# Small layernorm operations on GpSimd, paired feed-forward chunks, an earlier second load and a split last layernorm, in a two-layer graph network

## The chip, the cores and the metric

The kernel runs on one core of one Trainium2 chip. The metric is the device time of one execution in microseconds (us). The kernel before takes 3535.06 us, the median of three runs (3534.37 to 3538.44).

I call the engines by the short names that the profile uses: PE (TensorE, the matmuls), PEld (its weight loads), DVE (VectorE), ACT (ScalarE), POOL (GpSimd).

## The reference

The input is 128 graphs of 128 nodes with 256 features and an integer adjacency matrix each. Cut to what matters:

```python
def layer0(x, adj):
    h = gat(gat(x, adj, W1, a1), adj, W2, a2)      # two graph-attention steps: softmax over masked scores
    h = layernorm(x + h, g_ln1, b_ln1)
    ff = relu(h @ w_ff1 + b_ff1) @ w_ff2 + b_ff2    # 256 -> 1024 -> 256: the first feed-forward
    return layernorm(h + ff, g_ln2, b_ln2)

def layer1(src, adj):
    attn = softmax(q @ k.T / sqrt(32)) per head     # 8 heads, 4 relations that select values
    x = layernorm(src + attn_out @ Wo + bo, g1, beta1)
    ff = gelu(x @ W1 + b1) @ W2 + b2                # the second feed-forward
    return layernorm(x + ff, g2, beta2)
```

Everything is in float32. There are four layernorms per graph.

## The kernel before

The kernel works on 32 groups of four graphs and overlaps the stages of several groups: each stage is a generator, and a heap interleaves their steps by the begin and end times in a table. The build then orders the instructions of each engine by a simulated time, so the order on an engine is not simply the order of the text.

The layernorm of four graphs (128 calls in a run) takes its statistics on VectorE, `rstd` and `nmr` through three small operations that go from VectorE to GpSimd and back, and the scaling on ScalarE. The weights of the layernorm are applied by GpSimd, two operations for each pair of graphs (`affine`):

```python
def normalised(y):
    mv = sm.tile([P, G, 2], F32, name="mv")
    for b in range(G):
        st = sm.tile([P, 6], F32, name="st")
        nc.vector.bn_stats(st, y[:, b])
        nc.vector.bn_aggr(mv[:, b], st)
    rstd = sm.tile([P, G], F32, name="rstd")
    nc.vector.tensor_scalar(rstd, mv[:, :, 1], EPS, None, op0=OP.add)                                   # L166
    nc.gpsimd.tensor_tensor(rstd, rstd, mhalf, OP.pow)                                                  # L167
    nmr = sm.tile([P, G], F32, name="nmr")
    nc.vector.scalar_tensor_tensor(nmr, mv[:, :, 0], -1.0, rstd, op0=OP.mult, op1=OP.mult)              # L169
    for b in range(G):
        nc.scalar.activation(y[:, b], y[:, b], AF.Identity, bias=nmr[:, b:b + 1], scale=rstd[:, b:b + 1])  # L171

def affine(y, k, b):
    for op, v in zip((OP.mult, OP.add), ln[k][0]):
        nc.gpsimd.tensor_tensor(y[:, b:b + 2], y[:, b:b + 2], v[:, None, :].to_broadcast([P, 2, D]), op)   # L177
```

The feed-forward transposes its input, in two halves of 128 features. ScalarE writes the first half to `T` (L190) and VectorE the second (L188). Then come eight chunks of 128 hidden features, each with a matmul on either half (L202) into one accumulator tile "mm":

```python
def feed_forward(y, before, win, bin_, wout, func):
    hT = transposed(y, before)
    fT = []
    for f in range(FC):                                  # FC = 8
        p = ps.tile([P, T], F32, name="mm")
        for c in range(DC):                              # DC = 2, the halves
            nc.tensor.matmul(p, win[:, c, ts(f, P)], hT[:, c], start=c == 0, stop=c == DC - 1)   # L202
        t = wk.tile([P, T], F32, name="fT", tag="fT", bufs=FC + 1)
        nc.scalar.activation(t, p, func, bias=bin_[:, f:f + 1])                                  # L204
    ...                                                  # output matmuls (L214), add, normalised
```

Five accumulator tiles are called "mm", two "tr" and one "av": eight in all, each of 512 float32 columns or less. The Trainium skill ("PSUM — Partial Sum Buffer", the section "PSUM: the matmul accumulator") says that this is all there is, eight banks of 512 float32 values per partition.

Group 0's input is loaded among the first weights, group 1's behind all of them. The last group's output leaves in one piece, after the affine steps of all four graphs.

## Time and profile before

| | kernel before |
|---|---|
| time, median of 3 | 3535.06 us |
| span of the profiled run | 3533.7 us |
| PE busy | 3448.5 us (98%) |
| DVE, ACT, POOL busy | 49%, 48%, 31% |
| one group in the steady part | 108.02 us |

The last row is worked out from the trace: the distance between the first output matmuls (L214) of group 6's and of group 30's first feed-forward, over the 24 groups between (for these marks I count groups from 1; the code, and what I say of loading, counts from 0). With PE busy for 98% of the span, only its gaps can be won. The prediction below shows the lines for that. The two small operations that leave VectorE, each on its line of source; the columns are the count, then the shortest, median and longest duration in ns:

```profile
L166 DVE TENSOR_SCALAR rstd<-mv x128: 150/356/964, 43.8 to 3522.5; 128x4 f32<-128x4 f32 x128
L169 DVE SCALAR_TENSOR_TENSOR nmr<-mv,rstd x128: 133/164/1247, 45.1 to 3523.8; 128x4 f32<-128x4 f32 x128
```

Each is about 0.15 us of work at its shortest, and sometimes takes 1 us or more. The timeline of all engines shows such a case (start, duration, engine, line):

```profile
1082.43 1.28 POOL L177 TENSOR_TENSOR tok<-tok,ln_rows 128x512 f32<-128x512 f32 x1
1082.50 1.22 DVE L169 SCALAR_TENSOR_TENSOR nmr<-mv,rstd 128x4 f32<-128x4 f32 x1
```

The 4-column operation of VectorE begins just after GpSimd's large one and ends with it.

### The profile page before, as it was taken

Reading aid. Unit: us, or ns where it says so; the run is one execution under the profiler, and the core shown is the slowest. Engines: PE = TensorE matmul, PEld = TensorE weight load, DVE = VectorE, ACT = ScalarE, POOL = GpSimd, SP = SyncE. Lnnn points to the kernel's source line nnn. Section 1 sums busy time; section 2 is a strip of 40 time slices with the busy share of each in tenths; the row PEclk is TensorE's granted clock in tenths of the full one; section 3 lists DMA queues with packets and bytes.
Section 4 is the critical chain, followed back from the end, with each engine's and each line's share of the span. In section 5 each row is a group of like instructions: output and inputs, shape, how many; then the busy total and the mean of one; then the engine's idle time right before and its main releaser. Section 6 shows DMA issues by size and latency. Waiting matters only on the chain.

```text
span 3533.7 us, 52086 instructions
## 1 busy us (share of the span) xinstructions
PE 3448.5 (98%) x20496; PEld 2255.0 (64%) x20496; DVE 1720.9 (49%) x3781; ACT 1684.0 (48%) x4702; POOL 1091.0 (31%) x968
## 2 busy tenths in 40 slices
PE   7999999999999999999999999999999999999997
PEld 5566666666666666666666666666666666666655
DVE  2544445545455444455454554444554545544453
ACT  3455445555445554455554455544555544555442
POOL 2223323223233233232332332332323323323332
PEclk8999999999999999999999999999999999999999
DMA  4000000000000000000000000000000000000000
GB/s 177 7 10 22 22 22 16 7 22 22 22 16 13 16 22 22 22 16 7 22 22 22 16 11 18 22 22 22 16 7 22 22 22 10 9 8 7 7 7 13
DMA packets 23780, 70.86 MB, mean 20 GB/s; under 512 B 2416, under 2 KB 6000, under 8 KB 23408
## 3 DMA queue, kind: packets, MB, share of 16 engines
q1 hardware_dynamic: 23536, 67.53, 5.6%
q8 instruction: 162, 2.65, 0.3%
q14 instruction: 82, 0.67, 0.1%
HBM read 50.75 MB, written 16.78 MB: 19 GB/s over the span
## 4 chain that ended last, share of the span: by engine, by line
PE 85%; ACT 8%; DVE 5%; DMA 1%; issue 0%; POOL 0%; POOLq 0%; SPq 0%; ACTq 0%; DVEq 0%
PE mm L202 25%; PE mm L214 19%; PE mm L331 12%; PE av L343 7%; ACT kbd L286 5%; PE mm L246 3%; PE mm L277 3%; PE mm L370 3%; PE tr L318 3%; PE mm L295 2%; PE mm L255 2%; PE mm L264 2%; PE mm L283 2%; ACT e L233 1%; PE tr L186 1%; ACT tr L226 1%
## 5 line engine op out<-in xcount | busy, mean ns | idle before, releaser
L177 POOL TENSOR_TENSOR tok<-tok,ln_rows 128x512 f32<-128x512 f32 x512 | 640.2, 1276 | 442.8 <-PE tr L186 252.0
L322 DVE SCALAR_TENSOR_TENSOR m<-at,tr 128x512 f32<-128x512 int32 x1024 | 627.7, 678 | 93.6 <-PE tr L318 79.3
L307 POOL TENSOR_TENSOR e<-e,s 128x512 f32<-128x512 f32 x256 | 263.0, 1044 | 761.2 <-DVE mv L164 665.6
L204 ACT ACTIVATE fT<-mm,col 128x512 f32<-128x512 f32 x512 | 331.3, 686 | 339.4 <-PE mm L202 336.3
L202 PE MATMUL mm<-T,w 128*128 128x512 f32 x1024 | 476.0, 603 | 15.4 <-DVE T L188 14.8
L202 PE MATMUL mm<-T,wf 128*128 128x512 f32 x1024 | 471.1, 598 | 12.5 <-ACT T L190 12.5
L331 PE MATMUL mm<-wv,T 128*128 128x512 f32 x1024 | 461.0, 592 | 0.6 <-ACT e L305 0.6
L214 PE MATMUL mm<-w,fT 128*128 128x256 f32 x2048 | 460.3, 381 | 0.0
L214 PE MATMUL mm<-wf,fT 128*128 128x256 f32 x2048 | 456.0, 381 | 0.0
L171 ACT ACTIVATE tok<-tok,nmr,rstd 128x256 f32<-128x256 f32 x512 | 267.9, 611 | 377.2 <-DVE nmr L169 377.2
L215 DVE TENSOR_TENSOR tok<-tok,mm 128x512 f32<-128x512 f32 x128 | 88.0, 687 | 712.7 <-PE mm L214 712.7
L214 PEld LDWEIGHTS mm<-w,fT 128*128 128x128 f32 x2048 | 384.2, 190 | 69.4 <-issue 21.2
L214 PEld LDWEIGHTS mm<-wf,fT 128*128 128x128 f32 x2048 | 384.3, 190 | 57.1 <-issue 7.4
L305 ACT ACTIVATE e<-mm,nm 128x128 f32<-128x128 f32 x1024 | 358.6, 387 | 19.4 <-DVE nm L301 19.0
L202 PEld LDWEIGHTS mm<-T,w 128*128 128x128 f32 x1024 | 185.0, 190 | 234.4 <-issue 191.9
L202 PEld LDWEIGHTS mm<-T,wf 128*128 128x128 f32 x1024 | 184.6, 190 | 211.1 <-issue 184.0
L331 PEld LDWEIGHTS mm<-wv,T 128*128 128x128 f32 x1024 | 189.6, 190 | 203.3 <-issue 182.7
L235 POOL TENSOR_TENSOR e<-e,s 128x512 f32<-128x512 f32 x64 | 66.6, 1041 | 803.7 <-DVE s L234 803.7
L343 PEld LDWEIGHTS av<-m,v 128*32 128x32 f32 x8192 | 218.1, 110 | 70.8 <-issue 60.3
L167 POOL TENSOR_TENSOR rstd<-rstd,mhalf 128x4 f32<-128x4 f32 x128 | 130.2, 1017 | 430.9 <-DVE rstd L166 405.8
L343 PE MATMUL av<-m,v 128*32 128x128 f32 x8192 | 252.9, 276 | 7.8 <-DVE v L332 4.6
L347 ACT COPY oT<-av 128x256 f32<-128x256 f32 x128 | 47.0, 367 | 392.5 <-PE av L343 392.5
(62 smaller groups left out, 3897.9 us busy)
## 6 DMA issues: line engine op xcount, KB each, us to landing
xt<-in_xT_dram SPq DMA_DIRECT2D x32, 512.0 KB, 3.3
tok<-in_x_dram SPq DMA_DIRECT2D x32, 512.0 KB, 3.3
out_dram<-tok SPq DMA_DIRECT2D x32, 512.0 KB, 2.7
at<-in_adjT_dram SPq DMA_DIRECT2D x32, 256.0 KB, 2.8
wf<-in_wf_dram SPq DMA_DIRECT2D x2, 1024.0 KB, 10.6
w<-in_w_dram SPq DMA_DIRECT2D x2, 1024.0 KB, 13.0
ln_rows<-in_rows_dram SPq DMA_DIRECT2D x1, 1024.0 KB, 11.0
wv<-in_wv_dram SPq DMA_DIRECT2D x1, 1024.0 KB, 9.8
```

The costliest lines, as they stand in the source:

```text
L167: nc.gpsimd.tensor_tensor(rstd, rstd, mhalf, OP.pow)
L171: nc.scalar.activation(y[:, b], y[:, b], AF.Identity, bias=nmr[:, b:b + 1], scale=rstd[:, b:b + 1])
L177: nc.gpsimd.tensor_tensor(y[:, b:b + 2], y[:, b:b + 2], v[:, None, :].to_broadcast([P, 2, D]), op)
L202: nc.tensor.matmul(p, win[:, c, ts(f, P)], hT[:, c], start=c == 0, stop=c == DC - 1)
L204: nc.scalar.activation(t, p, func, bias=bin_[:, f:f + 1])
L214: nc.tensor.matmul(p[:, b - b2_], fT[f][:, ts(b, N)], wout[:, f], start=f == 0, stop=f == FC - 1)
L286: nc.scalar.activation(kbd[c][rows, :, q % 2], p[rows], AF.Identity, bias=bk[rows, c:c + 1])
L305: nc.scalar.activation(e[:, q], p[:, q], AF.Exp, bias=nm[:, q:q + 1], accum_out=s[:, q:q + 1])
L307: nc.gpsimd.tensor_mul(e, e, per_row(s, N))
L322: nc.vector.scalar_tensor_tensor(m, ab, r, pT, op0=OP.is_equal, op1=OP.mult)
L331: nc.tensor.matmul(p, hT[:, f, ts(b, N)], wv[:, f, r:r + 2], start=f == 0, stop=f == DC - 1)
L343: last = nc.tensor.matmul(po[ts(q, DH), c], v[:, r, c * P + q * DH:c * P + (q + 1) * DH], ms[q // 2][r][:, c * 2 + q % 2], start=r == R - ...
```

## The change

The intent, in four parts:

- **GpSimd:** all small operations of the layernorm go to GpSimd, so that VectorE no longer hands over and waits for the power.
- **Pairs:** the feed-forward takes its chunks by pairs, with the input half in the outer loop, so that two matmuls run on the first half before the second half is needed.
- **Loading:** the input of group 1 is loaded right behind the first weights.
- **End:** the last group is normalised and written out by two graphs at a time, with the affine steps on VectorE. In the same place the pauses (`yield 2`) before the affine steps of all other groups go too.

```diff
+    second_xt = ld.tile([P, DC, T], F32, name="xt")
+    nc.sync.dma_start(second_xt, xT[1])
...                                                   # at[1] beside it, x[1] before wf2; load_group from group 2 on
-    def normalised(y):
+    def normalised(y, first=0, n=G):
...
-        nc.vector.tensor_scalar(rstd, mv[:, :, 1], EPS, None, op0=OP.add)
-        nc.gpsimd.tensor_tensor(rstd, rstd, mhalf, OP.pow)
-        nmr = sm.tile([P, G], F32, name="nmr")
-        nc.vector.scalar_tensor_tensor(nmr, mv[:, :, 0], -1.0, rstd, op0=OP.mult, op1=OP.mult)
+        nc.gpsimd.tensor_scalar(rstd, mv[:, :, 1], EPS, None, op0=OP.add)
+        nmr = sm.tile([P, n], F32, name="nmr")
+        nc.gpsimd.tensor_scalar(nmr, mv[:, :, 0], -1.0, None, op0=OP.mult)
+        nc.gpsimd.tensor_tensor(rstd, rstd, mhalf[:, :n], OP.pow)
+        nc.gpsimd.tensor_mul(nmr, nmr, rstd)
...
-        for f in range(FC):
-            p = ps.tile([P, T], F32, name="mm")
+        for f0 in range(0, FC, 2):
+            pair = [ps.tile([P, T], F32, name="mm") for _ in range(2)]
             for c in range(DC):
-                nc.tensor.matmul(p, win[:, c, ts(f, P)], hT[:, c], start=c == 0, stop=c == DC - 1)
+                for i, p in enumerate(pair):
+                    nc.tensor.matmul(p, win[:, c, ts(f0 + i, P)], hT[:, c], start=c == 0, stop=c == DC - 1)
...
-        normalised(y)
+            if (b2_ + 2) % by == 0:                   # by = 2 in the last group's second feed-forward, else 4
+                normalised(y, b2_ + 2 - by, by)
...
+            affine(y, "12", b, nc.vector if last else nc.gpsimd)
+            if last:
+                nc.sync.dma_start(out[g][:, b:b + 2], y[:, b:b + 2])
...
-            if g == 1 and n < 2:
+            if g == 1 and n == 1:                     # group 1's first stage still begins 0.6 of a group early
```

More of the change, by code (lines that the diff above doesn't have):

```diff
@@ L106, in graph_layers @@
     nc.sync.dma_start(first_at, adjT[0])
+    second_xt = ld.tile([P, DC, T], F32, name="xt")
+    nc.sync.dma_start(second_xt, xT[1])
+    second_at = ld.tile([P, G, N], I32, name="at", bufs=4)
+    nc.sync.dma_start(second_at, adjT[1])
     first_x = wk.tile([P, G, D], F32, name="tok", bufs=KB)
     nc.sync.dma_start(first_x, x[0])
-    first_load = first_x, first_xt, first_at
     pa = ps.tile([P, DC, 2], F32, name="mm")
@@ L136, in graph_layers @@
           for n, k in enumerate(KS)}
+    second_x = wk.tile([P, G, D], F32, name="tok", bufs=KB)
+    nc.sync.dma_start(second_x, x[1])
     wf2 = wload("wf2")
@@ L156, in per_row @@
         return v[:, :, None].to_broadcast([P, v.shape[-1], n])
-    def normalised(y):
-        mv = sm.tile([P, G, 2], F32, name="mv")
-        for b in range(G):
+    def normalised(y, first=0, n=G):
+        y = y[:, first:first + n]
+        mv = sm.tile([P, n, 2], F32, name="mv")
+        for b in range(n):
             st = sm.tile([P, 6], F32, name="st")
@@ L164, in normalised, with affine @@
             nc.vector.bn_aggr(mv[:, b], st)
-        rstd = sm.tile([P, G], F32, name="rstd")
-        nc.vector.tensor_scalar(rstd, mv[:, :, 1], EPS, None, op0=OP.add)
-        nc.gpsimd.tensor_tensor(rstd, rstd, mhalf, OP.pow)
-        nmr = sm.tile([P, G], F32, name="nmr")
-        nc.vector.scalar_tensor_tensor(nmr, mv[:, :, 0], -1.0, rstd, op0=OP.mult, op1=OP.mult)
-        for b in range(G):
+        rstd = sm.tile([P, n], F32, name="rstd")
+        nc.gpsimd.tensor_scalar(rstd, mv[:, :, 1], EPS, None, op0=OP.add)
[3 more added lines that the diff above has]
+        nc.gpsimd.tensor_mul(nmr, nmr, rstd)
+        for b in range(n):
             nc.scalar.activation(y[:, b], y[:, b], AF.Identity, bias=nmr[:, b:b + 1], scale=rstd[:, b:b + 1])
-    def affine(y, k, b):
+    def affine(y, k, b, engine=nc.gpsimd):
         for op, v in zip((OP.mult, OP.add), ln[k][0]):
-            nc.gpsimd.tensor_tensor(y[:, b:b + 2], y[:, b:b + 2], v[:, None, :].to_broadcast([P, 2, D]), op)
+            engine.tensor_tensor(y[:, b:b + 2], y[:, b:b + 2], v[:, None, :].to_broadcast([P, 2, D]), op)
     def transposed(y, k):
@@ L191, in transposed, with feed_forward @@
         return t
-    def feed_forward(y, before, win, bin_, wout, func):
+    def feed_forward(y, before, win, bin_, wout, func, by=G):
         hT = transposed(y, before)
@@ L198, in feed_forward @@
         fT = []
-        for f in range(FC):
-            p = ps.tile([P, T], F32, name="mm")
+        for f0 in range(0, FC, 2):
+            pair = [ps.tile([P, T], F32, name="mm") for _ in range(2)]
             for c in range(DC):
-                nc.tensor.matmul(p, win[:, c, ts(f, P)], hT[:, c], start=c == 0, stop=c == DC - 1)
-            t = wk.tile([P, T], F32, name="fT", tag="fT", bufs=FC + 1)
-            nc.scalar.activation(t, p, func, bias=bin_[:, f:f + 1])
-            fT.append(t)
-            if f % 2:
-                yield 1
-                if f in (3, 5):
-                    affine(y, before, f - 3)
+                for i, p in enumerate(pair):
+                    nc.tensor.matmul(p, win[:, c, ts(f0 + i, P)], hT[:, c], start=c == 0, stop=c == DC - 1)
+            for i, p in enumerate(pair):
+                t = wk.tile([P, T], F32, name="fT", tag="fT", bufs=FC + 1)
+                nc.scalar.activation(t, p, func, bias=bin_[:, f0 + i:f0 + i + 1])
+                fT.append(t)
+            yield 1
+            if f0 in (2, 4):
+                affine(y, before, f0 - 2)
         for b2_ in range(0, G, 2):
@@ L376, in ff0, with ff1 @@
         return feed_forward(y, "01", wf1, bf1, wf2, AF.Relu)
-    def ff1(y):
-        return feed_forward(y, "11", w1, b1, w2, AF.Gelu)
-    x0, x1, x2, masks, loads = {}, {}, {}, {}, {0: first_load}
+    def ff1(y, by):
+        return feed_forward(y, "11", w1, b1, w2, AF.Gelu, by)
+    x0, x1, x2, masks, loads = {}, {}, {}, {}, {}
+    loads[0] = first_x, first_xt, first_at
+    loads[1] = second_x, second_xt, second_at
     def stage_load(g):
-        if g:
+        if g > 1:
             loads[g] = load_group(g)
@@ L399, in stage_ff1 @@
     def stage_ff1(g):
-        y = yield from ff1(x2.pop(g))
+        last = g == NG - 1
+        y = yield from ff1(x2.pop(g), 2 if last else G)
         for b in range(0, G, 2):
-            yield 2
-            affine(y, "12", b)
-        nc.sync.dma_start(out[g], y)
+            affine(y, "12", b, nc.vector if last else nc.gpsimd)
+            if last:
+                nc.sync.dma_start(out[g][:, b:b + 2], y[:, b:b + 2])
+        if not last:
+            nc.sync.dma_start(out[g], y)
     stages = ((stage_load, 1, -0.7, -0.6), (stage_gat, 11, 0.0, 0.5), (stage_ff0, 8.5, 0.65, 1.15),
```

## The prediction

> **What bounds the kernel now.** I read the page first, its engine totals:
>
> ```profile
> PE 3448.5 (98%) x20496; PEld 2255.0 (64%) x20496; DVE 1720.9 (49%) x3781; ACT 1684.0 (48%) x4702; POOL 1091.0 (31%) x968
> ```
>
> The matrix engine has work 98% of the time, the others at most half. All instructions that the change moves are on engines with room; they pay only where PE waits for them. PE is idle 3533.7 - 3448.5 = 85.2 us. Busy is not proof of full rate, so I next took the distance from one start to the next in the PE timeline:
>
> ```profile
> 1021.73 3.60 PE L331 MATMUL mm<-wv,T 128*128 128x512 f32 x8
> 1025.16 1.08 PE L186 MATMUL tr<-ident,tok 128*128 128x128 f32 x8
> 1026.63 2.84 PE L202 MATMUL mm<-T,wf 128*128 128x512 f32 x6 [0.39 <-ACT T L190]
> ```
>
> Eight 512-column instructions take 1025.16 - 1021.73 = 3.43 us, 0.429 us each; nearly all 512-column ones of the trace keep that pitch. (A feed-forward has 8 chunks x 2 halves x 32 groups = 512 matmuls and the trace 1024 instructions: two per matmul.) The change removes no matmul, so this rate is a floor, and only gaps can be won. Where they are, from the windows by stage:
>
> ```profile
> 0.00:54.00 54.00, 29.25 (x100) 22.55 (x101) 11.89 (x30) 20.14 (x62) 11.64 (x16) 0.81 0.79 290
> 54.00:215.00 161.00, 153.24 (x810) 101.43 (x808) 65.33 (x151) 68.72 (x190) 37.58 (x35) 0.98 0.03 9
> 215.00:3241.00 3026.00, 3000.78 (x17926) 1960.22 (x17922) 1508.27 (x3308) 1475.72 (x4123) 953.01 (x842) 1.00 0.05 17
> 3241.00:3486.00 245.00, 233.49 (x1562) 150.84 (x1562) 130.59 (x280) 107.73 (x311) 76.83 (x68) 1.00 0.02 7
> 3486.00:3534.00 48.00, 31.75 (x104) 19.97 (x104) 4.86 (x16) 11.71 (x18) 11.89 (x10) 0.84 0.03 11
> ```
>
> The second column is the length, the third PE's busy time, the third from the end its granted clock. Idle: start 24.8 us, filling 7.8, the 28 steady groups 25.2 (0.8%), emptying 11.5, end 16.3. And the list of waits of PE:
>
> ```profile
> PE mm L202 <- DVE T L188: 14.8, 29, 0.5
> PE mm L202 <- ACT T L190: 13.2, 32, 0.8
> PE tr L186 <- ACT tok L171: 8.6, 2, 5.3
> PE mm L255 <- POOL e L235: 6.0, 1, 6.0
> PE mm L246 <- DMA xt<-in_xT_dram: 5.3, 1, 5.3
> ```
>
> The two that repeat once per group are both the feed-forward's first matmuls, waiting for the transposed input: its first half comes from ScalarE (L190), its second from VectorE (L188). The change's outer loop over halves aims at these. The rest are single events of start and end.
>
> **What the skill says.** "TensorE: Matmul & The Clock Gate", Architectural detail: PE can pull a weight load ahead of running matmuls; its section on LDWEIGHTS gives columns / 1.2 GHz, 107 ns for 128. The trace agrees: where PE has stalled, the next instruction also comes 104 ns late (533 instead of 429 ns), so a stall costs its length and about one exposed load. Part 1 of that page: an idle array falls to half clock. Here the clock is 0.81 in the start and 0.84 in the end, so a shorter start gap is worth slightly more than itself. "SBUF — State Buffer", SBUF: two separate sides: VectorE with two SBUF inputs or in a two-port mode and GpSimd hold one port pair exclusively, the loser blocks. The trace is consistent: the 4-column VectorE operations of the layernorm take 0.17 us beside an idle GpSimd, but on average 0.469 (L166) and 0.665 us (L169). "GPSIMD Engine Reference", 4.1: elementwise is about 2x slower there; here 1.28 us for the 128x512 affine step, while VectorE adds 128x768 in 0.96 (L134).
>
> **The change, part by part.**
>
> *Pairs.* One steady group, from the timeline of all engines:
>
> ```profile
> 1079.23 0.66 DVE L301 TENSOR_REDUCE nm<-mm 128x4 f32<-128x512 f32 x1
> ...
> 1079.42 1.12 PE L202 MATMUL mm<-T,w 128*128 128x512 f32 x2
> ...
> 1079.80 0.50 DVE L166 TENSOR_SCALAR rstd<-mv 128x4 f32<-128x4 f32 x1
> ...
> 1080.21 0.80 DVE L188 TENSOR_SCALAR T<-tr,col 128x512 f32<-128x512 f32 x1
> ...
> 1081.07 2.84 PE L202 MATMUL mm<-T,w 128*128 128x512 f32 x6 [0.52 <-DVE T L188]
> ```
>
> The second feed-forward does one matmul on the first half, then needs the second, which VectorE evicts late, behind a maximum and the small L166. PE would have gone on at 1079.42 + 2 x 0.429 = 1080.28 (slightly later after its own exposed load, 0.10) and goes on at 1081.07: 0.69 us lost, and 0.10 after it, 0.79 per group. With pairs, a second matmul on the first half (2 x 0.429 = 0.86 us) comes before the second half is wanted, which covers all; and L166 leaves VectorE, so the half comes some 0.5 us earlier too. 30 groups x 0.79 = 24 us saved.
>
> The first feed-forward waits otherwise: for ScalarE's half, before its *first* matmul (the 1026.63 line above; 0.66 us with the exposed load after the last transpose). No loop order helps that. It also seems to run by pairs already: its second matmul starts at 1026.63 + 0.97 = 1027.60, while VectorE writes the second half from 1027.46 to 1028.23, so the build's scheduler must have put the next chunk's first-half matmul there. 0 us saved.
>
> *GpSimd.* 128 layernorms lose L166 and L169 from VectorE: 60.0 + 85.1 us of busy time and 118.8 us for which L169 held its queue waiting for the power. GpSimd gets three more 4-column operations, 384 in all. The trace has none except the power (1.02 us, a special function) and memsets (0.10 us); I estimate 0.15 us each, 58 us, 31% to 33% busy. The chain to ScalarE was 0.17 + 1.02 + 0.16 and two crossings, and becomes some 0.45 + 1.02 and one: equal. In the steady part PE does not wait for it: 0 us beyond the pairs' share.
>
> *Loading.* The PE timeline of the start:
>
> ```profile
> 16.33 0.95 PE L224 MATMUL tr<-ident,wh 128*128 128x128 f32 x4
> 23.29 3.69 PE L255 MATMUL mm<-wh,e 128*128 128x258 f32 x8 [6.01 <-POOL e L235]
> 26.82 0.95 PE L224 MATMUL tr<-ident,wh 128*128 128x128 f32 x4
> 33.03 5.70 PE L246 MATMUL mm<-wx,xt 128*128 128x260 f32 x16 [5.27 <-DMA xt<-in_xT_dram]
> 38.57 1.03 PE L264 MATMUL mm<-wh,e 128*128 128x256 f32 x4
> ```
>
> Group 1's input was issued behind all weights, and its 16 matmuls stand in PE's queue ahead of group 0's L264, whose weights were ready near 33.7 (GpSimd's L235 at 32.68 + 1.04). Issued sixth, it lands near 11 us (estimate from the first loads, 512 KB in about 1.3 us), so those matmuls fit the gap at 17 to 23, or at worst start at 27.7. L264 then starts near 34 instead of 38.6, less about 0.5 us of crowding on ScalarE: 4.5 us. Group 1's own chain runs some 10 us earlier, so its later gat steps fill the 5.3 us gap before group 0's transposes and about 4 us of them no longer stand between these and the first feed-forward. I take 9 us in all, at least 4, at most 14.
>
> *End.* After the last PE instruction (3520.7) come add, statistics, power, ScalarE's scaling, then
>
> ```profile
> 3525.25 4.92 POOL L177 TENSOR_TENSOR tok<-tok,ln_rows 128x512 f32<-128x512 f32 x4 [1.46 <-ACT tok L171]
> 3530.20 0.33 SPq L404 DMA_DIRECT2D out_dram<-tok  x1
> ```
>
> By two graphs, the first half is normalised under the second half's matmuls. For the last half: add 0.7, statistics 1.0, GpSimd about 1.5, two scalings 1.15 ending near 3525.2, two affine steps on VectorE at about 0.68 to 3526.6, then half the output, 3.5 us before, about 3.1: 3529.7. Saved 4 us, less up to 1 if the first half's affine stands before the last add in VectorE's queue.
>
> Sum: 24 + 9 + 4 = 37 us. I keep 2 us for small new waits: 3535 - 35 = 3500.
>
> **Rivals.** *A new stall per group.* The order of instructions comes from a simulated time at build; new small operations shift it, and any place may now stall. One stall of the size seen, 0.66 to 0.79 us x 31, costs 20 to 25 us: 3520 to 3525. For it: both existing stalls are of this kind. Against: no other wait of PE repeats now. *PSUM.* A pair holds two of five "mm" banks through 3.4 us; if ScalarE, crowded by exponentials (L305), evicts late, the next pair waits. An eviction takes 0.686 us, against 1.72 us of matmul per chunk, and the pairs of the first feed-forward already work. A wait of 0.3 us on 256 pairs would give +77, 3577; unlikely. *GpSimd as the brake.* If a 4-column operation costs 1 us rather than 0.15, GpSimd rises by 384 us to 42%, still no bound, but a layernorm ends 3 us later; start and end lose some 6 us and steady PE little: 3506. *The first stall goes too,* if other work gets placed before the first feed-forward: 21 us more, 3479.
>
> **Range and chances.** The steady 24 us is well supported (29 waits alike), the start is uncertain by 5, the schedule by about 20 on either side. Range 3480 to 3524. Faster by 2% means below 3464.4, which would need almost all of the 85 us idle; slower means above 3605.8, for which only the PSUM rival at double size reaches. Hence 0.03, 0.94, 0.03.
>
> **What would show it.** L202's wait for L188 gone from the waits of PE; its wait for L190 still there, 32 times, about 13 us; steady idle down from 25 us towards 11; one steady period shorter by 0.79 us. L246 of group 1 before 28 us with no wait for a load, L264 near 34. The span ending about 9 us after the last matmul instead of 13. VectorE busy down by about 145 us. I am wrong if a wait of PE appears some 30 times that is not in the list now, or if the second half's wait survives the pairs.

## More of the kernel before

The scores of the attention (L295), which ScalarE turns into exponentials (L305), use "mm" tiles too.

The waits of the weight loads (PEld), which are a list of their own (total us, times, longest):

```profile
PEld mm L202 <- DVE T L188: 45.7, 58, 1.3
PEld mm L255 <- ACT fT L204: 8.1, 29, 0.3
```

The first belongs to the second half of the transposed input, which VectorE writes. The second is a graph-attention matmul that waits for ScalarE to empty an accumulator of the feed-forward.

The lines shift by a few: L188, L190, L202, L204, L214 of before are L195, L197, L210, L213, L222 of after.

## The result, and the profile after

The changed kernel takes 3510.07 us, the median of six runs (3508.11 to 3510.62), beside 3536.53 us for six runs of the kernel before (3534.37 to 3538.66). The ratio is 0.9925, with a 95% interval from 0.9912 to 0.9937. A ratio here is the mean time of one kernel's fast runs over that of the other's of the same rounds, so it is not quite the ratio of the quoted medians. The prediction was 3500 us in a range of 3480 to 3524, so the time came out 10 us above it and inside the range. All outputs are right.

The engine totals of the changed kernel, and its windows by stage (length, then busy time of PE, PEld, DVE, ACT and POOL, then clock, DMA share, GB/s):

```profile
PE 3442.3 (98%) x20496; PEld 2256.7 (64%) x20496; DVE 1602.0 (46%) x3529; ACT 1692.8 (48%) x4702; POOL 1167.7 (33%) x1352
```

```profile
0.00:54.00 54.00, 32.21 (x101) 23.42 (x102) 13.29 (x31) 20.65 (x66) 12.22 (x19) 0.78 0.79 290
...
215.00:3241.00 3026.00, 3012.29 (x18050) 1973.18 (x18049) 1407.25 (x3100) 1501.86 (x4181) 1033.21 (x1188) 1.00 0.05 17
```

In the steady window PE's idle time fell from 25.2 to 3026 - 3012.3 = 13.7 us, near the 11 that the prediction named. The first line of the list of waits of PE:

```profile
PE mm L210 <- ACT T L197: 12.3, 31, 0.7
```

The wait for VectorE's half, 14.8 us in 29 pieces before, is gone from this list, and the wait for ScalarE's half is still there, 31 times. So far this is what the prediction said. But the list of the weight loads shows the wait for VectorE again:

```profile
PEld mm L210 <- DVE T L195: 34.2, 59, 0.9
```

It was 45.7 us and 58 times before. The wait has shrunk and has not gone. (A wait of a weight load is not all lost to PE; what PE lost per group is worked out below.) To see where the time went I took some marks in the two traces (start of the first of the output matmuls, in us):

| mark | before | after | difference |
|---|---|---|---|
| first feed-forward of group 1 of 32 | 68.03 | 67.44 | -0.6 |
| of group 5 | 402.45 | 398.86 | -3.6 |
| of group 31 | 3211.03 | 3189.51 | -21.5 |
| last second feed-forward | 3506.68 | 3482.58 | -24.1 |
| end of the span | 3533.7 | 3506.2 | -27.5 |

From group 5 to group 31 the gain is 17.9 us in 26 periods, 0.69 us each; the period is 107.333 us instead of 108.023. The prediction had 0.79. The end gives 3.4 us, where it had 4. The start gives 0.6 us, where it had 9. The sum is close to the prediction; whether the parts did what it said, the experiments must show.

### The profile page after: what moved, and what is told of

It reads as the page before. It is cut to its first block, busy times and chain, and to the rows that moved or that the text cites. A ratio compares the mean times of both kernels' runs of the same rounds, so it can differ in the third digit from the quotient of the medians.

```text
span 3506.2 us, 52290 instructions
## 1 busy us (share of the span) xinstructions
PE 3442.3 (98%) x20496; PEld 2256.7 (64%) x20496; DVE 1602.0 (46%) x3529; ACT 1692.8 (48%) x4702; POOL 1167.7 (33%) x1352
## 4 chain that ended last, share of the span: by engine, by line
PE 85%; ACT 9%; DVE 5%; issue 1%; POOL 0%; DMA 0%; SPq 0%; ACTq 0%; POOLq 0%; DVEq 0%
PE mm L210 25%; PE mm L222 20%; PE mm L340 12%; PE av L352 7%; ACT kbd L295 5%; PE mm L255 3%; PE mm L286 3%; PE mm L379 3%; PE tr L327 3%; PE mm L304 2%; PE mm L273 2%; PE mm L292 2%; PE mm L264 2%; ACT e L242 2%; PE tr L193 1%; ACT tr L235 1%
## 5 line engine op out<-in xcount | busy, mean ns | idle before, releaser
L213 ACT ACTIVATE fT<-mm,col 128x512 f32<-128x512 f32 x512 | 337.9, 687 | 331.4 <-PE mm L210 327.4
L210 PE MATMUL mm<-T,wf 128*128 128x512 f32 x1024 | 473.7, 601 | 11.7 <-ACT T L197 11.7
L210 PE MATMUL mm<-T,w 128*128 128x512 f32 x1024 | 476.4, 604 | 3.6 <-ACT T L197 0.7
L222 PE MATMUL mm<-w,fT 128*128 128x256 f32 x2048 | 460.3, 381 | 0.0
L222 PE MATMUL mm<-wf,fT 128*128 128x256 f32 x2048 | 456.0, 381 | 0.0
L222 PEld LDWEIGHTS mm<-w,fT 128*128 128x128 f32 x2048 | 384.2, 190 | 69.7 <-issue 21.5
L223 DVE TENSOR_TENSOR tok<-tok,mm 128x512 f32<-128x512 f32 x128 | 88.0, 687 | 733.5 <-PE mm L222 730.5
L222 PEld LDWEIGHTS mm<-wf,fT 128*128 128x128 f32 x2048 | 384.3, 190 | 57.1 <-issue 7.4
L210 PEld LDWEIGHTS mm<-T,w 128*128 128x128 f32 x1024 | 182.9, 190 | 221.0 <-issue 184.9
L210 PEld LDWEIGHTS mm<-T,wf 128*128 128x128 f32 x1024 | 185.9, 191 | 212.9 <-issue 186.6
L314 ACT ACTIVATION_READ_ACCUMULATOR e<-mm,nm 128x1 f32 x1024 | 231.9, 226 | 0.0
```

The source lines that it names most:

```text
L210: nc.tensor.matmul(p, win[:, c, ts(f0 + i, P)], hT[:, c], start=c == 0, stop=c == DC - 1)
L213: nc.scalar.activation(t, p, func, bias=bin_[:, f0 + i:f0 + i + 1])
L222: nc.tensor.matmul(p[:, b - b2_], fT[f][:, ts(b, N)], wout[:, f], start=f == 0, stop=f == FC - 1)
L314: nc.scalar.activation(e[:, q], p[:, q], AF.Exp, bias=nm[:, q:q + 1], accum_out=s[:, q:q + 1])
```

## The experiments

### Each part alone

Four kernels, each the kernel before with one part of the change. The first moves the small operations and nothing else:

```diff
-        nc.vector.tensor_scalar(rstd, mv[:, :, 1], EPS, None, op0=OP.add)
-        nc.gpsimd.tensor_tensor(rstd, rstd, mhalf, OP.pow)
+        nc.gpsimd.tensor_scalar(rstd, mv[:, :, 1], EPS, None, op0=OP.add)
-        nc.vector.scalar_tensor_tensor(nmr, mv[:, :, 0], -1.0, rstd, op0=OP.mult, op1=OP.mult)
+        nc.gpsimd.tensor_scalar(nmr, mv[:, :, 0], -1.0, None, op0=OP.mult)
+        nc.gpsimd.tensor_tensor(rstd, rstd, mhalf, OP.pow)
+        nc.gpsimd.tensor_mul(nmr, nmr, rstd)
```

> The kernel before with one part of the change: the small layernorm operations on GpSimd. On record the prediction gave this part 0 us in the steady groups (3536, ratio 1.000), since the pairs were to cover the wait alone. The rival, formed from the trace after: the first feed-forward matmuls of the second feed-forward still run unpaired there and still wait for VectorE's half, only about 0.41 us less per group, the time in which L166 stood ahead of that half in VectorE's queue. Then this part alone should shorten the steady period from 108.02 us by 0.4 to 0.7 us, 12 to 21 us in all: ratio 0.994 to 0.9965.

The second has only the pairs (the third hunk of the diff above):

```diff
-        for f in range(FC):
-            p = ps.tile([P, T], F32, name="mm")
+        for f0 in range(0, FC, 2):
+            pair = [ps.tile([P, T], F32, name="mm") for _ in range(2)]
```

> The kernel before with the pairs alone. The prediction gave them 24 us (0.79 us in 30 groups): ratio 0.993. The rival: the first pair is not run as a pair, since four of the five mm banks hold attention scores, so the wait for VectorE's half stays at about 0.67 us and the ratio is 0.999 to 1.001.

The third loads group 1 early:

```diff
+    second_xt = ld.tile([P, DC, T], F32, name="xt")
+    nc.sync.dma_start(second_xt, xT[1])
```

> The kernel before with the second group's loads first. The prediction gave this 9 us (ratio 0.9975) by group 0's second weighted sum starting near 34 us instead of 38.6. The rival, from the trace after: it starts at 38.1, since group 1's chain now shares ScalarE and VectorE with group 0's and delays it; the first feed-forward's output matmuls start only 0.6 us earlier. Then the ratio is 0.9995 to 1.000.

The fourth splits the last layernorm, with the small operations as they were:

```diff
+            affine(y, "12", b, nc.vector if last else nc.gpsimd)
+            if last:
+                nc.sync.dma_start(out[g][:, b:b + 2], y[:, b:b + 2])
```

> The kernel before with the last layernorm by two graphs, the last affine step on VectorE, and the affine steps of the other groups issued at once after the layernorm. The prediction gave it 4 us less up to 1 (ratio 0.9989 to 0.9992); both theories agree here. If moving the affine steps of the other groups matters, the steady period changes from 108.02 us and the ratio leaves 0.998 to 1.000.

All four ran beside nine runs of the kernel before with a median of 3539.53 us. These nine lay in two clusters (3534.5 to 3535.9 and 3540.0 to 3540.5, with one at 3539.5), so I rest on the traces more than on the last few microseconds of the times.

| run | median us | ratio, 95% interval | period us | first output matmul | from the last output matmuls to the end |
|---|---|---|---|---|---|
| before | 3539.53 | | 108.023 | 68.03 | 27.02 |
| pool_only | 3513.44 | 0.9929 (0.9917 to 0.9941) | 107.333 | 69.26 | 27.38 |
| pairs_only | 3535.77 | 0.9996 (0.9983 to 1.0008) | 108.005 | 68.90 | 27.02 |
| load_only | 3532.84 | 0.9984 (0.9972 to 0.9997) | 108.005 | 66.99 | 27.02 |
| tail_only | 3532.01 | 0.9981 (0.9967 to 0.9995) | 108.024 | 69.08 | 22.95 |
| changed kernel | 3510.07 | 0.9925 (0.9912 to 0.9937) | 107.333 | 67.44 | 23.64 |

(The marks of "before" are those of its first profile.) The whole steady gain comes from the GpSimd part, for which the prediction had put down 0 us. The pairs, for which it had put down 24 us, do nothing: period 108.005 us, and in PE's list the wait still stands:

```profile
PE mm L203 <- DVE T L188: 14.7, 29, 0.5
```

The GpSimd part alone and the whole change agree not only in the period but in each kind of instruction. I added up the distances from each PE start to the next over the same 24 groups, by tiles: no kind differs by more than 0.001 us per group between the two. The end works as predicted, 27.02 to 22.95 us. The first output matmul scatters by 2 us among runs that load nothing earlier (67.37 in eps_only, which comes next, to 69.26), so at this mark what loading gives (66.99 alone, 67.44 in the changed kernel) is hardly clear of the scatter.

### Which of the small operations matters

If VectorE's queue was what kept the second half back, moving L166 alone should do it. Two kernels, each the kernel before with one half of the GpSimd part:

```diff
-        nc.vector.tensor_scalar(rstd, mv[:, :, 1], EPS, None, op0=OP.add)
+        nc.gpsimd.tensor_scalar(rstd, mv[:, :, 1], EPS, None, op0=OP.add)
```

> The kernel before, with only the addition of EPS (L166) moved from VectorE to GpSimd; L169 stays on VectorE. Theory A: what counts is L166's place in VectorE's queue, ahead of the eviction of the second half. Then the lost time before that half falls from 0.67 to about 0.26 us per group, the steady period from 108.02 to between 107.33 and 107.6 us, the ratio to 0.993 to 0.9965. Theory B: what counts is L169, which held VectorE's queue while it waited for the power; then this run keeps 108.02 us and a ratio of 0.999 to 1.001.

```diff
-        nc.gpsimd.tensor_tensor(rstd, rstd, mhalf, OP.pow)
-        nc.vector.scalar_tensor_tensor(nmr, mv[:, :, 0], -1.0, rstd, op0=OP.mult, op1=OP.mult)
+        nc.gpsimd.tensor_scalar(nmr, mv[:, :, 0], -1.0, None, op0=OP.mult)
+        nc.gpsimd.tensor_tensor(rstd, rstd, mhalf, OP.pow)
+        nc.gpsimd.tensor_mul(nmr, nmr, rstd)
```

> The kernel before, with only the product of mean and reciprocal deviation (L169) moved to GpSimd, as two operations; L166 stays on VectorE. Theory A: the lost time before the second half stays at about 0.67 us; the steady period stays near 108.0 us, or 107.8 if the 0.24 us that the change also saved before the gat weighted sums belong to L169. Theory B: the period falls to 107.3 to 107.6 us and the ratio to 0.993 to 0.9965.

Beside 3535.81 us for before, eps_only took 3534.64 us (ratio 0.9997, 0.9982 to 1.0012) and nmr_only 3548.16 us (1.0037, 1.0022 to 1.0052). Neither half gives the gain, and one of them loses 0.30 us per group: their periods are 108.005 and 108.322 us. Neither theory fits both: A missed both periods, though the half did come earlier in eps_only, and B had that of eps_only right and missed that of nmr_only. The distances from start to start say why. The table has all places where the sum per group differs from before by over 0.01 us; a place is the instruction behind which PE came late:

| us per group, against before | second feed-forward's matmuls on `T` | graph-attention matmuls into `mm` (L255) | transposes of the exponentials, just ahead of L255 | sum |
|---|---|---|---|---|
| pool_only, changed kernel | -0.41 | -0.25 | -0.04 | -0.69 |
| eps_only | -0.41 | 0.00 | +0.39 | -0.02 |
| nmr_only | +0.58 | -0.25 | -0.04 | +0.30 |

In eps_only the second half does come earlier, and PE gains the 0.41 us. But a few microseconds later it waits for ScalarE in place of it, at L255, in 29 groups:

```profile
PE mm L255 <- ACT fT L204: 7.7, 29, 0.3
```

L255 needs a free accumulator, and ScalarE frees it when it evicts the feed-forward's first chunks (`fT`). In before and in eps_only ScalarE does its four layernorm scalings first and the evictions then: 5.3 and 8.8 us after the start of the second feed-forward's matmuls, medians of 20 groups. In one group of before:

```profile
1084.76 2.15 ACT L171 ACTIVATE tok<-tok,nmr,rstd 128x256 f32<-128x256 f32 x4
...
1088.21 1.27 ACT L204 ACTIVATE fT<-mm,col 128x512 f32<-128x512 f32 x2
```

ScalarE's order has not moved in eps_only, so PE, 0.41 us earlier, only waits longer for it. In pool_only, nmr_only and the changed kernel the order is the other way round: evictions 6.8 to 7.0 us and scalings 8.3 to 8.6 us after that start. In the changed kernel:

```profile
1078.53 1.26 ACT L213 ACTIVATE fT<-mm,col 128x512 f32<-128x512 f32 x2
...
1080.32 2.08 ACT L178 ACTIVATE tok<-tok,nmr,rstd 128x256 f32<-128x256 f32 x4 [0.53 <-POOL nmr L176]
```

The operation that moved with them is `nmr`: with L169 on GpSimd the build places the scalings later and the evictions earlier. That takes the 0.25 us away, and lets the 0.41 us through.

In nmr_only L166 stays on VectorE, and GpSimd begins its affine step before it. L166 then takes 1.09 us in the group that I looked at (0.50 us in the one of before), and the second half, which stands behind it, comes late:

```profile
PE mm L203 <- DVE T L189: 32.1, 30, 1.1
```

So the two moves are worth something only together. The first frees VectorE's queue and the second ScalarE's order.

### Why the pairs do nothing

In the changed kernel the timeline of all engines around the second feed-forward of one group reads:

```profile
1071.70 4.07 PE L210 MATMUL mm<-T,w 128*128 128x512 f32 x8
...
1072.07 0.80 DVE L195 TENSOR_SCALAR T<-tr,col 128x512 f32<-128x512 f32 x1
...
1072.56 0.37 ACT L314 ACTIVATE e<-mm,nm 128x128 f32<-128x128 f32 x1
```

VectorE's half now starts 0.37 us after PE's first matmul (1072.07 - 1071.70); before, with L166 ahead of it, it started 0.79 us after (1080.21 - 1079.42). That is the 0.42 us. The merged line of PE shows no wait, but hides one: eight instructions without any would take 0.533 + 6 x 0.429 + 0.592 = 3.70 us (the first distance has a weight load exposed, 0.592 is the modelled length of the last), and they take 4.07. The missing 0.37 us is what is left of the stall, a wait of 0.27 us and the 0.10 us of the weight load after it.

A pair would put a second chunk's matmul there. In the order of the build it isn't there: the first chunk's two matmuls come first, then the second chunk's, as if there were no pairs. My reason was that the second chunk needs another accumulator. Four of the five hold attention scores at this time, and the first comes free when ScalarE ends the fourth exponential, near 1072.56 + 0.37 = 1072.93. VectorE's half is ready at 1072.07 + 0.80 = 1072.87. So the pair could not start before the second half was there anyway.

First I tried the pair where accumulators might be free. Both kernels are the changed kernel with the second feed-forward begun 0.1 of a group earlier, with and without pairs:

```diff
-              (stage_attention, 16, 2.0, 3.0), (stage_ff1, 8.5, 3.15, 3.65))
+              (stage_attention, 16, 2.0, 3.0), (stage_ff1, 8.5, 3.05, 3.55))
```

> The changed kernel with the second feed-forward of each group begun a little earlier in the interleaving (3.05 instead of 3.15), so that its first chunks come before the second graph's attention scores, when mm banks are free, and the build lays the first pair out as a pair. If the pairs failed for want of a bank, the second half's wait (0.26 us and 0.10 after it per group in the changed kernel) is now 0 here. Compared with the next run, which differs only in the pairs, the loss at that place should be at least 0.3 us per group smaller. If instead pairs cannot cover this wait at all, it is the same in both. The period itself may differ from 107.33 us by other effects of the earlier place.

> The same earlier place without the pairs (the loop of before). Here the first chunk's second matmul waits for VectorE's half: some 0.3 to 0.9 us lost per group at that place, and the time longer than that of early_pairs by as much times 30, 9 to 27 us, if the theory of the banks holds.

They took 3846.48 us (ratio 1.0879, clock 0.972) and 3939.44 us (1.1143, clock 0.963), with periods of 118.85 and 121.88 us. These don't answer the question. The second half was in time in both, so there was no wait for a pair to cover, and the pairs were ahead by 3 us per group for another reason (without pairs the matmuls for the values waited 73.7 us in all for an accumulator, with pairs they did not, and the feed-forward waited 33.0 us). What they do show is how sharply this kernel hangs on its interleaving: with the pairs, a shift of a tenth of a group cost 9.6% against the changed kernel (3846.48 against 3510.07 us).

A better test leaves the interleaving as it is and lets ScalarE evict the second half of this feed-forward. Then the build does lay the first pair as a pair, and PE must show what the second chunk waits for:

```diff
-            if c % 2:
+            if c % 2 and k != "11":
                 nc.vector.tensor_scalar(t[:, c], p, gain[:, c:c + 1], offset[:, c:c + 1], op0=OP.mult, op1=OP.add)
```

> The changed kernel, but the second half of the second feed-forward's transposed input is evicted by ScalarE instead of VectorE. In this build the first pair of that feed-forward does run as a pair (both chunks on the first half, then both on the second). It asks whether the missing accumulator bank is what kept the pair from helping. Theory (bank): the second chunk's first matmul comes 0.86 us after the first one, about 1072.56 on the clock of the group that I looked at, and must wait for ScalarE's fourth exponential to free the bank near 1073.0; so a wait of PE for ScalarE's e of 0.3 to 0.5 us stands there some 30 times in place of the 0.37 us for VectorE, and the period stays within 0.2 us of 107.33 (time 3505 to 3516). Rival (loop order): the pair alone covers the second half's eviction, as the prediction had it; then no wait is left there and the period falls to about 106.95 (time about 3498).

It took 3514.56 us (ratio 0.9936, 0.9921 to 0.9951, beside 3538.05 for before), with a period of 107.487 us. The timeline and PE's list:

```profile
1072.71 1.12 PE L210 MATMUL mm<-T,w 128*128 128x512 f32 x2
...
1074.08 1.13 PE L210 MATMUL mm<-T,w 128*128 128x512 f32 x2 [0.25 <-ACT e L314]
```

```profile
PE mm L210 <- ACT e L314: 7.4, 29, 0.3
```

PE does the first chunk's matmul on the first half (two instructions) and then waits, no longer for `T` but for an exponential, 29 times. From start to start the third instruction is 0.42 us late and the next, with its weight load, 0.10 us: 0.52 us for the accumulator in place of 0.37 us for VectorE, which makes 107.333 + 0.15 = 107.48 us. The period says 107.487. Nor can it be the second half that the third instruction waits for: it starts at 1074.08, and ScalarE writes that half from 1073.91 to 1074.70. The bank theory holds and the loop order alone does not cover the eviction. Once the accumulator is free the pair does cover it: the second half's first matmul follows at the full pitch of 0.429 us, after 1074.70. No run gave the pair a free accumulator in an otherwise unchanged kernel, so what it would save then is not shown.

### Trying to take the rest

Could the transposed input come earlier? This is the changed kernel with a higher priority for the transposes and their evictions, so that they go ahead of scores and maxima:

```diff
-        hT = transposed(y, before)
+        with tc.high_priority(offset=1000):
+            hT = transposed(y, before)
```

> The changed kernel, with the transposes and evictions at the head of both feed-forwards given a higher priority at build, so that they come ahead of the attention scores and their maxima in the queues. Theory: what PE still waits for at the two feed-forwards (0.37 us per group at the second, 0.66 us at the first) is only the place of these evictions in the queues; brought forward, at least the second one's wait goes: period 106.3 to 107.0, time 3480 to 3500. Rival: what they displace (scores, maxima, exponentials) comes late instead, and a new wait of PE of 0.4 us or more appears some 30 times: period 107.3 or longer, time 3508 or longer.

It took 3528.64 us (ratio 0.9976, 0.9961 to 0.9991; period 108.210). My expectation missed and its rival came true. VectorE's half no longer comes late, and PE waits for the accumulator instead (the list has `ACT e`, 11.5 us in 29 pieces). By start-to-start distances the second feed-forward's matmuls took 0.30 us per group more than in the changed kernel, the attention scores 0.42 us and the graph-attention matmuls that were L255 0.16 us: together 0.88 us, the whole difference of the periods.

### The start

The prediction expected group 1's first matmuls to fill PE's gap from 17 to 23 us, and the first group's L264 (L273 now) near 34. The PE timeline of the changed kernel's start:

```profile
23.55 3.56 PE L264 MATMUL mm<-wh,e 128*128 128x258 f32 x8 [6.76 <-POOL e L244]
26.95 1.04 PE L255 MATMUL mm<-wx,xt 128*128 128x260 f32 x4
27.82 0.27 PE L233 MATMUL tr<-ident,wh 128*128 128x128 f32 x1
...
38.08 3.78 PE L273 MATMUL mm<-wh,e 128*128 128x256 f32 x8 [6.34 <-POOL e L244]
...
49.95 12.49 PE L210 MATMUL mm<-T,wf 128*128 128x512 f32 x24
```

The load is no longer waited for, as predicted, but group 1's matmuls (L255) stand behind group 0's L264 in PE's order, and leave the gap open. Behind it they come between group 0's transposes (L233), which end at 31 us instead of 28. The rest of group 0's chain moves with them, so L273 starts at 38.08 us (38.57 before). The first feed-forward then begins at 49.95 instead of 52.57 us, but with a granted clock of 0.60 between 50 and 55 us, where the kernel before had 1.00 between 52.5 and 57.5 us: its 24 instructions take 12.49 us instead of 10.46. So 2.6 us won became 0.6.

To fill the gap after all, group 1's first stage begins still earlier:

```diff
             if g == 1 and n == 1:
-                begin, end = begin - 0.6, end - 0.6
+                begin, end = begin - 0.9, end - 0.9
```

> The changed kernel, with the second group's first stage begun 0.3 of a group earlier in the interleaving, so that its sixteen first matmuls stand in PE's order ahead of the first group's L264. Steady part and end unchanged: period 107.33. Theory of the start (the matmuls stood behind L264 and so did not fill PE's gap from 17 to 23 us): now they fill it, the first feed-forward's output matmuls begin 2 to 5 us earlier than 67.44, time 3505 to 3508. Rival (the start is bound by the chain of transposes, leaky ReLU, maxima and exponentials over ScalarE and VectorE, which both groups now share): filling PE's gap gives under 1 us, or the two chains crowd each other more and it gets later than 67.44.

It took 3512.37 us (ratio 0.993, 0.9913 to 0.9946; period 107.331). The matmuls of group 1 (sixteen instructions, two per matmul) now do stand in the gap, from 14.8 to 18.7 us:

```profile
25.91 4.67 PE L264 MATMUL mm<-wh,e 128*128 128x258 f32 x10 [6.29 <-POOL e L244]
```

Yet group 0's L264 comes 2.4 us later than in the changed kernel (25.91 against 23.55), and the first output matmul at 73.36 us instead of 67.44. So filling the gap gained nothing, as the rival said. Where the first 2.4 us went, the timelines show: group 0's own transposes (L233) now stand between group 1's matmuls in PE's order, the last at 18.66 us instead of 16.47, and ScalarE begins on them at 19.14 instead of 16.84. From there to L264 the chain over ScalarE, VectorE and GpSimd takes 6.8 us, as it did (6.7). The other 3.5 us I did not take apart; that the two groups crowd each other on those engines is the rival's reason, and is not shown for them.

The last run has both edits:

> The changed kernel with both of the previous two edits: higher priority for the feed-forwards' transposed input, and the second group begun earlier. If the two act in different stages, as I think, its gain over the changed kernel is the sum of theirs to within 2 us. If T_hp_all is slower, this is slower too.

It took 3535.32 us (ratio 0.9995, 0.9981 to 1.001), 25 us above the changed kernel's 3510.07; the two edits alone were 18.6 and 2.3 us above it. The sum, 20.9, misses by 4.4 us where I had allowed 2, so the two are not quite independent (the changed kernel's time is of another call, in which before had 3536.53 us instead of 3538.05): the start got later still (74.75 us), while the period was that of T_hp_all, 108.210 us.

None of these beat the changed kernel, which stays the fastest of all that I ran.

## Why the prediction was right, and where it was wrong

**The time and the range** were right: 3510 in 3480 to 3524, and "within 2%".

**"30 groups x 0.79 = 24 us saved" by the pairs** is the step that failed. The stall was read correctly: 0.67 us of lateness at the second half's first instruction and 0.10 us after it, in the start-to-start distances. What failed was "With pairs, a second matmul on the first half ... comes before the second half is wanted, which covers all". It took an accumulator for granted that the attention scores hold. The prediction did name PSUM as a rival, but only for later pairs and late evictions, not for the first pair beside the scores. The runs with the pairs alone and with the ScalarE eviction show this. By the prediction's own sign ("or if the second half's wait survives the pairs") it was wrong here: 0.67 us of lateness with the pairs alone, 0.27 us in the changed kernel.

**"In the steady part PE does not wait for it: 0 us beyond the pairs' share"** for the GpSimd part failed too. It gave all of the 0.69 us per group. The prediction had half of the mechanism in its own text: "L166 leaves VectorE, so the half comes some 0.5 us earlier too" (measured 0.42 us). It booked this under the pairs, which would have hidden it. The other half it had not seen: ScalarE's order of scalings and evictions, and the wait at L255 that is only in the list of the weight loads. That the two wrong terms nearly cancelled (24 and 0 against 0 and 0.69 x 30 = 20.7) was luck.

**"I take 9 us in all"** for the loading failed: 0.6 us by the first output matmul, 1 us in the run of this part alone, neither clear of the scatter. The named assumption was that PE's gap at 17 to 23 us would be filled, or that L264 would start near 34 anyway. Neither happened, and the run in which the gap was filled was later. The remark that "a shorter start gap is worth slightly more than itself" did not come true either: the clock of the first 54 us fell from 0.81 to 0.78, and the first feed-forward, begun earlier, ran in the slower part.

**"Saved 4 us, less up to 1"** for the end was right: 27.02 - 23.64 = 3.4 us. The timeline of the changed kernel shows the suspected order:

```profile
3496.38 0.69 DVE L184 TENSOR_TENSOR tok<-tok,ln_rows 128x512 f32<-128x512 f32 x1 [2.74 <-ACT tok L178]
3496.98 0.68 DVE L223 TENSOR_TENSOR tok<-tok,mm 128x512 f32<-128x512 f32 x1
3497.58 0.68 DVE L184 TENSOR_TENSOR tok<-tok,ln_rows 128x512 f32<-128x512 f32 x1
```

The last add (L223) stands between the two affine steps of the first half, and the statistics of the second half behind both. The run with the end alone, where small operations stayed on VectorE, gained 4.1 us. PE's last output matmuls run to 3482.58 + 13.98 = 3496.56, and the span ends 9.7 us later; "about 9" was predicted.

**The price of the small operations** was set too low. The prediction's estimate was 0.15 us each; the profile after gives:

```profile
L172 POOL TENSOR_SCALAR rstd<-mv x129: 232/233/247, 43.7 to 3499.2; 128x4 f32<-128x4 f32 x127, 128x2 f32<-128x2 f32 x2
```

The other two take 0.225 and 0.202 us (medians). GpSimd rose by 76.7 us instead of 58, to 33%, which is the predicted share. VectorE fell by 118.9 us, where the two rows removed add up to 145; a row counts an instruction's whole span, and spans overlap.

**What stays open.** That ScalarE's order flips with L169's move is what the three runs with it and the two without it show. Why the build's ordering reacts like this I only infer: `nmr` seems to be expected later. I also did not run the changed kernel without its pairs; that they are worth nothing beside the GpSimd part rests on pool_only having the same period and the same distances. And the 3 us between groups 1 and 5 are only partly the steady gain of 0.69 us per group; I did not take the filling apart.

## What to carry to other kernels

A loop order that covers a late operand needs a free accumulator at that very moment, so look at who holds the banks before counting the gain. Read the list of the weight loads and the start-to-start distances beside the list of PE's waits, because a stall under a matmul's modelled end can show only there, as the waits at L210 in the changed kernel and at L255 in the kernel before did. And test each part alone: a total that agrees with the prediction can hide that one part did the other's work.

## What the Trainium skill lacked or had wrong

- "GPSIMD Engine Reference", section 4.1, compares elementwise work on whole tiles and gives no price for tiny operands. Here a 4-column add or multiply took 0.20 to 0.23 us, beside 0.13 to 0.17 us on VectorE while GpSimd is idle, and the power on 4 columns 1.04 us, on 2 columns 0.71 us.
- "SBUF — State Buffer" says that the loser of the shared port pair fully blocks (its Terms, and "SBUF: two separate sides"). The runs agree: a 4-column VectorE operation of 0.15 us took up to 1.25 us beside a GpSimd operation of 1.28 us. What the page has no example of is the cost to a third engine: in nmr_only one such operation in front of an eviction made PE wait 32.1 us in 30 pieces, through all that was queued behind it.
- "TensorE: Matmul & The Clock Gate", section on LDWEIGHTS, gives columns / 1.2 GHz, about 107 ns for 128 columns (an estimate from its formula). Nothing is wrong here: after a stall the runs show the next instruction 104 ns late.
